# Moving the query scales, merging the copies of key scales, and writing out the order in which an attention opens

## The chip, the cores and the metric

The kernel runs on one core of a Trainium2 chip. The core has five engines that run side by side and wait for each other by semaphores: TensorE (PE; PEld is its weight load), VectorE (DVE), ScalarE (ACT), GpSimd (POOL) and SyncE (SP). DMA transfers are issued from queues on SP, POOL and ACT. The metric is the device time of one execution in microseconds (us). For the kernel before, three runs gave 2776.56, 2783.22 and 2783.88; the median is 2783.22. One more execution was recorded by the profiler.

## The reference, cut to what matters

The model is one block of a perceiver: cross attention to a long context, causal self attention, and a gated feed-forward layer with 4-bit weights. The change touches the cross attention. There, 512 rows of queries (4 x 128 tokens) meet 8192 keys (4 x 2048), in 16 heads of 64 columns, with queries, keys, values and attention weights rounded to integers:

```python
q = (x @ Wq + bq).reshape(1, B * N, H, hd)
kv = (cond @ Wkv + bkv).reshape(1, -1, 2, H, hd)
k, v = (kv[:, :, 0], kv[:, :, 1])
scale = 1.0 / np.sqrt(hd).astype(np.float32)
...
q = _fq_sym(q, axis=-1)          # one scale for each query and head
k = _fq_sym(k, axis=-1)          # one scale for each key and head
v = _fq_sym(v, axis=2)           # one scale for each column
attn = jnp.einsum('bhqd,bhkd->bhqk', q, k)
attn = jax.nn.softmax(attn.astype(jnp.float32), axis=-1)
attn = _fq_unsigned(attn, axis=-1)
out = jnp.einsum('bhqk,bhkd->bhqd', attn, v)
...
return out @ Wp + bp
```

`_fq_sym` divides by a scale (the largest magnitude over 127), rounds, and multiplies back. The kernel keeps the rounded integers and the scales apart.

## The kernel before, in words

The context's 8192 tokens are cut into 64 tiles of 128 tokens (`KT`). A first pass projects them to values (steps 0 to 63), a second pass to keys (steps 64 to 127). One step is one tile: its two halves of 512 columns each take 24 matmuls (`project`, line 364), since every fp32 product is made from three products of split operands. VectorE joins the two accumulators of a half (`join`, lines 378 and 379). In the second pass it then quantises the half (`quantise_k`, by `quantise`: lines 197 to 205): maximum magnitude, scale `sk`, its reciprocal `rs`, and the integers `ki`. SP transposes `ki` by DMA into `kT` (line 630), ScalarE casts that into `kst` (line 644), and POOL stores it to the DRAM buffer `k_d` (line 651).

After every 16 tiles (a key chunk of 2048 keys, four in all) `key_scales` (line 658) turns that chunk's scales into rows: two TensorE transposes (line 663), one for even and one for odd tiles, each into a PSUM tile of its own, a copy from each to `sk_row` (line 665; by ScalarE, for the last chunk by VectorE), and a store to `sk_d` by POOL (line 666). These PSUM tiles come from the same ring of eight as the accumulators.

The order of both passes is written out: `do(step, fn)` puts a piece of work at a step, and `perform()` issues all of it sorted by step, inside `tc.manual_schedule()`, which keeps each engine's instructions in the order of issue. Outside such a block a scheduler places them.

While the last tile of keys is worked on, `open_keys` opens the pool `keys` in the memory of a closed pool, on the right side of the on-chip memory. It holds the keys of a head (`kt`, line 677), the key scales as one row (`sk_half`, line 691) and the same scales spread over all partitions (`sk`, line 696, by POOL). Chunks 0 to 2 are loaded and spread in the written order; the last chunk follows at the opening of the attention (lines 991 to 995), outside the manual block, along with the first load of scale rows for head 1 (`load_rows`, line 833) and the value scales `sv` (line 995). Before these lines, also under the scheduler, the kernel makes `sqs` in the pool `small` from the query scales `sq`: a reciprocal (line 817) and three multiples (line 819). `sqs` gives the exponential its scale and the maximum its operands. An identity matrix is cast to fp16 (line 821).

The attention itself is a written order again: 64 units (16 heads by 4 query tiles), 8 steps of 1024 keys each. In a step TensorE makes scores (line 857), VectorE multiplies them by the spread key scales into `e` and keeps the maximum (line 864). After 8 steps VectorE forms the row's maximum `m` (line 880), ScalarE takes the exponential of `e` in two halves of 4096 (line 898, three buffers of `e`), and later TensorE (line 913) or DMA (line 929) transposes the result, which meets the values (line 962; loaded by POOL, line 827). POOL adds the two sums of the exponentials at the end of a head (line 971).

When the last scores have been issued, `open_projection` (line 1007) closes the pools on the right side, `keys` among them, opens new ones in their place, and has POOL load the first output weights `wp` in two halves (line 1026) and rows of `x` (line 1031). `first_step` (line 1046) begins the output projection with them, between the last transposes and values of the attention:

Of the kernel before, what the change touches and what calls it, by code (L numbers as in the profile page):

```python
# [34 lines left out]
F32 = mybir.dt.float32  # L35
# [5 lines left out]
AF = mybir.ActivationFunctionType  # L41
# [5 lines left out]
P = 128  # L47
B, S, C = 4, 128, 1024
NT = B * S // P
NC = C // P  # L50
H, D = 16, 64
# [3 lines left out]
KT = NK // P  # L55
# [33 lines left out]
def tile_perceiver(  # L89
# [146 lines left out]
    def do(step, fn, *args):  # L236
        agenda.append((step, len(agenda), fn, args))
# [339 lines left out]
    kv = {}  # L577
# [54 lines left out]
    def in_order(t, c):  # L632

        dims = "p h" if len(t.shape) == 3 else "p"
        if c in DMA_KC:
            return t.rearrange(f"{dims} (e n) -> {dims} n e", e=2)
        return t.rearrange(f"{dims} (n e) -> {dims} n e", e=2)
# [20 lines left out]
    def key_scales(c):  # L658

        row = pools["k"].tile([P, 2 * P], F32, name="sk_row", tag="sk_row", bufs=1)  # L660
        for e in range(2):
            pt = kv_ps.tile([P, P], F32, name="sk_pt", tag="ps")
            nc.tensor.transpose(pt, sks[c].rearrange("p h (i e) -> p e h i", e=2)[:, e], ident)
            copy = nc.scalar.copy if c < NKC - 1 else nc.vector.tensor_copy
            copy(in_order(row, c)[:, :, e], pt)
        nc.gpsimd.dma_start(out=sk_d[c].rearrange("h (i n) -> (h i) n", n=2 * P), in_=row)

    kts, sks_at = {}, {}

    def open_keys():  # L670

        early_s.close()
        pools["keys"] = xq.enter_context(tc.tile_pool(name="at_k", bufs=1, side="right"))

    def load_keys(h, c):
        kt = pools["keys"].tile([P, KC // 2], BF16, name=f"kt{h}_{c}", tag="kt", bufs=6)
        nc.sync.dma_start(out=kt, in_=k_d[c][h].rearrange("f d n -> (f d) n"))
        kts[h, c] = kt
# [5 lines left out]
    def load_scales(c):  # L684

        if c == 0:
            sks_at["rows"] = pools["keys"].tile([P, SC], F32, name="sk_half")
        row = sks_at["rows"]
        for half in range(2):
            p = 32 * (2 * (c % 2) + half)  # L690
            nc.sync.dma_start(out=row[p : p + 1, :], in_=sk_d[c][0:1, ts(half, SC)])

    def spread_first(c):
        for half in range(2):
            p = 32 * (2 * (c % 2) + half)
            nc.gpsimd.partition_broadcast(
                tile_of_scales(0, 2 * c + half), sks_at["rows"][p : p + 1, :], channels=P
            )
# [80 lines left out]
    for u in range(first, last):  # L779
        at = TILE * (KT + u)  # L780
        upto = -(-KT * (u + 1 - first) // (last - first))
        for i, v in enumerate(range(done, upto)):
            do(at + 8 + 6 * i, quantise_v, v)
            do(at + 10 + 6.2 * i, store_v, v)
        done = upto
    at = TILE * (2 * KT - 1)
    do(at + 0.2, open_keys)
    for c in range(NKC - 1):
# [19 lines left out]
    with tc.tile_pool(name="at_e", bufs=1) as at_e, tc.tile_pool(  # L808
# [4 lines left out]
        sc_ps = sc_s.enter_context(tc.tile_pool(name="sc_ps", bufs=2, space=PSUM, side="right"))  # L813
        sv = small.tile([P, C], F32, name="sv", tag="sv", bufs=1)

        sqs = small.tile([P, 3, NT, H], F32, name="sqs", tag="sqs", bufs=1)
        nc.vector.reciprocal(sqs[:, 2], sq)
        for i, by in enumerate((1.0, -1.0, -math.log(255.0))):
            nc.vector.tensor_scalar_mul(sqs[:, i], sqs[:, 2] if i == 2 else sq, by)
        ident16 = small.tile([P, P], F16, name="ident16", tag="ident16", bufs=1)  # L820
        nc.scalar.copy(ident16, ident)
        vqs = {}

        def load_values(p, c):
# [163 lines left out]
                scale.tensor_tensor(o, o, r.unsqueeze(2).to_broadcast([P, NT, D]), ALU.mult)  # L988


        load_scales(NKC - 1)
        load_keys(0, NKC - 1)
        spread_first(NKC - 1)
        load_rows(1)
        nc.sync.dma_start(out=sv, in_=sv_d[0].partition_broadcast(P))

        n_steps = len(units) * NSC

# [706 lines left out]
```

## Time and profile before

| what | us |
|---|---|
| median of three runs | 2783.22 |
| the profiled execution | 2784.63 |
| its span | 2782.9 |
| PE busy | 2599.6 (93%) |
| DVE busy | 2402.1 (86%) |
| ACT busy | 1259.2 (45%) |
| POOL busy | 513.5 (18%) |

The span runs from the first to the last recorded instruction of the profiled execution; the rest of its time lies around it. In the profile, "out<-in" names what an instruction writes and reads, L with a number is a line of the kernel before, and brackets after an instruction tell how long its engine stood idle ahead of it and what ended that. Roughly, the queries and values are projected until 750 us, the keys until 1478 us, the cross attention runs until 2100 us, and the rest follows until the end. The mean granted TensorE clock was 0.989 of full speed.

### The profile page before, as it was taken

The page shows a single profiled execution, that of the slowest core. Times are in us where ns is not written, and L with a number is a line of the kernel's source. Part 1 is how long each engine was busy: PE and PEld are TensorE (multiplying, and loading weights), DVE is VectorE, ACT ScalarE, POOL GpSimd, SP SyncE. Part 2 cuts the span into 40 slices and gives each one's busy share as a digit, 9 for nine tenths or more (in the row PEclk, how much of TensorE's full clock was granted, in tenths as well). Part 3 has the DMA queues.
Part 4 walks back from the last instruction along what each step waited for, and adds up shares of the span by engine and source line. Part 5 has one row for each costly group of instructions (what it writes and reads, how often), then busy time and mean ns, then how long its engine had stood idle before and what let it go on. Part 6 is the DMA issues. An engine that isn't in the chain of part 4 may idle for free.

```text
span 2782.9 us, 41479 instructions
## 1 busy us (share of the span) xinstructions
PE 2599.6 (93%) x15496; PEld 2054.8 (74%) x15496; DVE 2402.1 (86%) x3932; ACT 1259.2 (45%) x1404; POOL 513.5 (18%) x715
## 2 busy tenths in 40 slices
PE   8999999999999999999997777777779999899998
PEld 4888888888878788888884555555556777788887
DVE  7999999777899899999878999999995568886685
ACT  4211112222323333333216999999994134333332
POOL 0111111111112222222114333333322000000000
PEclk9999999999999999999998999999999999999999
DMA  6655566788747777777636888888887741133222
GB/s 200 193 201 195 195 232 227 262 296 283 266 109 196 184 190 199 193 192 192 143 84 150 169 171 158 164 158 171 166 156 236 287 156 61 53 99 99 99 93 97
DMA packets 470203, 485.05 MB, mean 174 GB/s; under 512 B 357096, under 2 KB 361768, under 8 KB 470000
## 3 DMA queue, kind: packets, MB, share of 16 engines
q1 hardware_dynamic: 411920, 286.04, 41.2%
q0 software_dynamic: 57024, 195.30, 21.3%
q8 instruction: 122, 2.00, 0.3%
q10 hardware_dynamic: 1056, 1.05, 0.2%
q14 instruction: 81, 0.66, 0.1%
HBM read 256.31 MB, written 140.51 MB: 143 GB/s over the span
## 4 chain that ended last, share of the span: by engine, by line
PE 68%; DVE 24%; issue 4%; DMA 3%; ACT 1%; DVEq 0%; POOL 0%; SPq 0%; ACTq 0%; POOLq 0%
PE kv_a L364 29%; DVE e L864 16%; PE kv_b L364 14%; PE acc_a L1215 4%; PE y_a L1592 3%; PE up_a L180 3%; PE gate_a L180 3%; PE q_ps L314 2%; PE acc_b L1215 2%; PE up_b L180 1%; PE gate_b L180 1%; PE y_b L1592 1%; PE a_pt L913 1%; PE acc_a L1046 1%; DMA sw_d<-ws_d 1%
## 5 line engine op out<-in xcount | busy, mean ns | idle before, releaser
L364 PE MATMUL kv_a<-w_h,c_h 128*128 128x512 f32 x2048 | 798.6, 390 | 0.0
L364 PE MATMUL kv_a<-w_l,c_l 128*128 128x512 f32 x2048 | 797.9, 390 | 0.7 <-ACT w_l L263 0.6
L364 PE MATMUL kv_b<-w_d,c_d 128*128 128x512 f32 x2048 | 797.8, 390 | 0.8 <-DVE c_d L174 0.8
L864 DVE CUSTOM_DVE_ANT_0 e<-sc,sk 128x1024 f32<-128x1024 f32 x512 | 592.0, 1218 | 2.0 <-PE sc L857 1.1
L898 ACT ACTIVATE a<-e,m,sqs 128x4096 int16<-128x4096 f32 x128 | 490.2, 3830 | 5.3 <-DVE m L880 4.9
L364 PEld LDWEIGHTS kv_a<-w_l,c_l 128*128 128x128 f32 x2048 | 385.1, 188 | 81.5 <-ACT w_l L263 1.0
L364 PEld LDWEIGHTS kv_b<-w_d,c_d 128*128 128x128 f32 x2048 | 385.0, 188 | 81.2 <-DVE c_d L174 1.1
L364 PEld LDWEIGHTS kv_a<-w_h,c_h 128*128 128x128 f32 x2048 | 385.2, 188 | 80.3 <-issue 0.2
L857 PE MATMUL sc<-kt,qT 64*128 64x512 bf16 x1024 | 204.6, 390 | 132.8 <-DVE mx L864 131.0
L378 DVE SCALAR_TENSOR_TENSOR f<-kv_a,bkv 128x512 f32<-128x512 f32 x256 | 175.3, 685 | 93.3 <-PE kv_a L364 92.7
L170 ACT ACTIVATE c_h<-c_raw 128x1024 fp32r<-128x1024 f32 x128 | 134.9, 1054 | 224.0 <-PE kv_a L364 199.9
L644 ACT CAST kst<-kT 128x512 bf16<-128x512 int16 x128 | 89.1, 697 | 304.7 <-DMA kT<-ki 304.7
L386 ACT ACTIVATE va<-f 128x1024 f32<-128x1024 f32 x64 | 68.0, 1062 | 302.4 <-DVE f L379 296.7
L857 PEld LDWEIGHTS <-qT 64*128 64x128 bf16 x1024 | 76.9, 93 | 160.6 <-issue 132.9
L379 DVE SCALAR_TENSOR_TENSOR f<-kv_b,f 128x512 f32<-128x512 f32 x256 | 176.5, 689 | 19.2 <-DVE f L378 0.5
L913 PE MATMUL a_pt<-ident,a 128*128 128x128 f32 x1024 | 170.2, 289 | 2.1 <-ACT aT L920 1.3
L837 POOL PARTITION_BROADCAST sk<-sk_row x120 | 142.5, 1299 | 129.7 <-DVE mx L864 129.4
L173 DVE TENSOR_TENSOR c_l<-c_raw,c_h 128x1024 fp32r<-128x1024 f32 x128 | 155.6, 1216 | 9.1 <-ACT c_h L170 9.1
L174 DVE SCALAR_TENSOR_TENSOR c_d<-c_l,c_raw 128x1024 fp32r<-128x1024 f32 x128 | 156.4, 1222 | 3.1
L173 DVE TENSOR_TENSOR fw_l<-fw_raw,fw_h 128x1024 fp32r<-128x1024 f32 x64 | 78.2, 1222 | 91.3 <-ACT fw_h L170 91.3
L913 PEld LDWEIGHTS a_pt<-ident,a 128*128 128x128 f32 x1024 | 109.0, 142 | 61.2 <-issue 42.7
L170 ACT ACTIVATE fw_h<-fw_raw 128x1024 fp32r<-128x1024 f32 x64 | 67.9, 1061 | 165.8 <-PE y_a L1592 69.5
(221 smaller groups left out, 4133.5 us busy)
## 6 DMA issues: line engine op xcount, KB each, us to landing
c_raw<-in_ctxT SPq DMA_DIRECT2D x128, 512.0 KB, 3.8
v_d<-f POOLq DMA_DIRECT2D x64, 512.0 KB, 3.4
vl<-v_d POOLq DMA_DIRECT2D x64, 512.0 KB, 4.5
gu_d<-w_ffn POOLq DMA_DIRECT2D x44, 512.0 KB, 3.2
fw_raw<-gu_d SPq DMA_DIRECT2D x42, 512.0 KB, 3.2
k_d<-kst POOLq DMA_DIRECT2D x128, 128.0 KB, 3.5
vq_d<-vq POOLq DMA_DIRECT2D x32, 512.0 KB, 5.2
kt<-k_d SPq DMA_DIRECT2D x64, 256.0 KB, 6.8
```

What stands on the lines that cost most here:

```text
L170: nc.scalar.mul(hi, src, 1.0 - 0.5 / UP)
L173: nc.vector.tensor_tensor(lo, src, hi, ALU.subtract)
L174: nc.vector.scalar_tensor_tensor(df, lo, -1.0 - UP, src, ALU.mult, ALU.add)
L180: nc.tensor.matmul(ps, lhsT=lhs(i, k), rhs=rhs(i, k), start=(k == 0 and i != 1), stop=(k == NC - 1 and i != 0),)
L364: nc.tensor.matmul(ps, lhsT=tokens[s][i][:, k, :], rhs=w3[s < KT][k][i][:, ts(n, 512)], start=(k == 0 and i != 1), stop=(k == NC - 1 and i ...
L378: nc.vector.scalar_tensor_tensor(f, a, 1.0 + 1.0 / UP, bias[s < KT][n], ALU.mult, ALU.add)
L379: nc.vector.scalar_tensor_tensor(f, b, -1.0 / UP, f, ALU.mult, ALU.add)
L857: nc.tensor.matmul(ps[:, ts(i, 512)], lhsT=qT[rows, h, ts(t, P)], rhs=kts[h, g // 2][rows, ts(g % 2, 512)], start=True, stop=True,)
L864: nc.vector.tensor_tensor_reduce(out=state[n]["e"][-1][:, ts(g % (NSC // NEC), SC)], in0=ps, in1=sks_at[h, g], scale=1.0, scalar=LOWEST, o ...
L898: nc.scalar.activation(a, st["e"][c], AF.Exp, bias=st["m"], scale=sqs[:, 0, t, h : h + 1], accum_out=sums[h][:, t, c : c + 1],)
L913: nc.tensor.transpose(pt[:, i, :], a[:, at_word + P * i : at_word + P * i + P], ident)
L1215: nc.tensor.matmul(ps, lhsT=x3[i][:, t, k, :], rhs=w3s[h, k // 2][i][:, k % 2, :], start=(k == 0 and i != 1), stop=(k == NC - 1 and i != 0),)
```

## The change

There are three edits.

1. `sqs` is made by a new function `scales_of_q`, put into the written order at the step at which the last tile of keys begins. It no longer lies in the pool `small` but in the pool `keys`.
2. `key_scales` makes both transposes into one PSUM tile and copies it to `sk_row` in one instruction.
3. The opening of the attention stands in a `tc.manual_schedule()` block, and after its loads come the cast of the identity and a new exponential of one column into a tile `table`, which makes ScalarE load its table of exponentials there.

```diff
     def key_scales(c):
 
         row = pools["k"].tile([P, 2 * P], F32, name="sk_row", tag="sk_row", bufs=1)
+        pt = kv_ps.tile([P, 2, P], F32, name="sk_pt", tag="ps")
         for e in range(2):
-            pt = kv_ps.tile([P, P], F32, name="sk_pt", tag="ps")
-            nc.tensor.transpose(pt, sks[c].rearrange("p h (i e) -> p e h i", e=2)[:, e], ident)
-            copy = nc.scalar.copy if c < NKC - 1 else nc.vector.tensor_copy
-            copy(in_order(row, c)[:, :, e], pt)
+            nc.tensor.transpose(
+                pt[:, e], sks[c].rearrange("p h (i e) -> p e h i", e=2)[:, e], ident
+            )
+        copy = nc.scalar.copy if c < NKC - 1 else nc.vector.tensor_copy
+        copy(in_order(row, c), pt.rearrange("p e n -> p n e"))
         nc.gpsimd.dma_start(out=sk_d[c].rearrange("h (i n) -> (h i) n", n=2 * P), in_=row)
+
+    def scales_of_q():
+        sqs = kv["sqs"]
+        nc.vector.reciprocal(sqs[:, 2], sq)
+        for i, by in enumerate((1.0, -1.0, -math.log(255.0))):
+            nc.vector.tensor_scalar_mul(sqs[:, i], sqs[:, 2] if i == 2 else sq, by)
 
...
         early_s.close()
         pools["keys"] = xq.enter_context(tc.tile_pool(name="at_k", bufs=1, side="right"))
+        kv["sqs"] = pools["keys"].tile([P, 3, NT, H], F32, name="sqs")
...
         done = upto
+    do(TILE * (2 * KT - 1) + 1, scales_of_q)
     at = TILE * (2 * KT - 1)
     do(at + 0.2, open_keys)
...
-        sqs = small.tile([P, 3, NT, H], F32, name="sqs", tag="sqs", bufs=1)
-        nc.vector.reciprocal(sqs[:, 2], sq)
-        for i, by in enumerate((1.0, -1.0, -math.log(255.0))):
-            nc.vector.tensor_scalar_mul(sqs[:, i], sqs[:, 2] if i == 2 else sq, by)
         ident16 = small.tile([P, P], F16, name="ident16", tag="ident16", bufs=1)
-        nc.scalar.copy(ident16, ident)
+        sqs = kv["sqs"]
+        table = small.tile([P, 1], F32, name="table", tag="table", bufs=1)
...
-        load_scales(NKC - 1)
-        load_keys(0, NKC - 1)
-        spread_first(NKC - 1)
-        load_rows(1)
-        nc.sync.dma_start(out=sv, in_=sv_d[0].partition_broadcast(P))
+        with tc.manual_schedule():
+            load_scales(NKC - 1)
+            load_keys(0, NKC - 1)
+            spread_first(NKC - 1)
+            load_rows(1)
+            nc.sync.dma_start(out=sv, in_=sv_d[0].partition_broadcast(P))
+            nc.scalar.copy(ident16, ident)
+            nc.scalar.activation(table, ident[:, 0:1], AF.Exp)
```

## The prediction

> **What bounds the kernel now.** I read the chain of work that ended last first, then the same chain in order of time around the two places that the change reaches (the start of the attention near 1475 us, its end near 2100 us), then the timeline of each engine there. The first answer says who carries the time as a whole:
>
> ```profile
> PE 68%; DVE 24%; issue 4%; DMA 3%; ACT 1%; DVEq 0%; POOL 0%; SPq 0%; ACTq 0%; POOLq 0%
> ```
>
> Before 1472 us and after 2100 us the chain is almost all TensorE; in the attention it is VectorE (line 864). So microseconds won or lost at a hand-over between stages pass to the end unless a later wait absorbs them. This is VectorE's timeline at the first hand-over (start, duration, then in brackets what it waited for):
>
> ```profile
> 1462.07 0.69 DVE L379 SCALAR_TENSOR_TENSOR f<-kv_b,f 128x512 f32<-128x512 f32 x1
> ...
> 1463.96 0.69 DVE L205 TENSOR_TENSOR ki<-f,rs 128x512 int16<-128x512 f32 x1
> ...
> 1466.71 0.69 DVE L378 SCALAR_TENSOR_TENSOR f<-kv_a,bkv 128x512 f32<-128x512 f32 x1 [2.06 <-PE kv_a L364]
> ...
> 1472.95 0.69 DVE L379 SCALAR_TENSOR_TENSOR f<-kv_b,f 128x512 f32<-128x512 f32 x1
> 1473.56 0.54 DVE L817 RECIPROCAL sqs<-sq 128x64 f32<-128x64 f32 x1
> ...
> 1474.57 0.78 DVE L819 TENSOR_SCALAR sqs<-sq 128x64 f32<-128x64 f32 x2
> 1475.19 1.32 DVE L200 TENSOR_SCALAR sk<-am 128x8 f32<-128x8 f32 x1
> 1476.29 0.26 DVE L819 TENSOR_SCALAR sqs<-sqs 128x64 f32<-128x64 f32 x1
> ...
> 1476.79 0.69 DVE L205 TENSOR_TENSOR ki<-f,rs 128x512 int16<-128x512 f32 x1
> 1477.40 0.48 DVE L665 COPY sk_row<-sk_pt 128x128 f32<-128x128 f32 x2
> 1478.69 1.23 DVE L864 CUSTOM_DVE_ANT_0 e<-sc,sk 128x1024 f32<-128x1024 f32 x1 [0.81 <-PE sc L857]
> ...
> 1493.65 1.23 DVE L864 CUSTOM_DVE_ANT_0 e<-sc,sk 128x1024 f32<-128x1024 f32 x1 [0.86 <-ACT a L898]
> ```
>
> The four scale instructions were drawn between the last half tile's quantisation steps: line 379 to line 205 takes 3.84 us there (1472.95 to 1476.79) and 1.89 us two half tiles earlier (1462.07 to 1463.96). The last line is a stall that starts with ScalarE: its timeline has a 1.28 us load of the exponential's table at 1488.43, after the first maximum. The second hand-over, POOL, ScalarE and TensorE:
>
> ```profile
> 2095.32 1.72 POOL L1026 DMA_DIRECT2D wp<-in_xWp  x2 [15.89 <-DVE m L880]
> 2099.18 3.80 ACT L898 ACTIVATE a<-e,m,sqs 128x4096 int16<-128x4096 f32 x1
> 2102.87 0.20 ACT L898 ACTIVATION_READ_ACCUMULATOR a<-e,m,sqs 128x1 f32 x1
> 2102.92 2.05 PE L1046 MATMUL acc_a<-wp,x 128*128 128x512 f32 x2 [2.69 <-DMA wp<-in_xWp]
> ```
>
> The weights wp are requested as the last maximum ends, fly 7.5 us, and TensorE stands 2.69 us for them. This load is on the chain already, and it starts before the last exponential has run.
>
> **The change, part by part.**
>
> *Scales of queries.* Four instructions leave the last half tile and go after the join before, where VectorE waits 2.06 us for TensorE. They take 0.54 + 0.78 + 0.26 = 1.6 us, less as they overlap, so the gap holds them. The quantisation there ends near 1466.1 instead of 1464.65; its transpose leaves SP at 1467.35, behind two scale loads that wait for POOL, so nothing is late. If the gap were gone the cost would be those 1.6 us at most. In the last half tile line 205 starts 1.95 us earlier, at 1474.84.
>
> *One tile and one copy for key scales.* Two copies of 128 columns took 0.48 us; one took 0.28, a 512-column VectorE pass 0.69, so one of 256 lies between 0.28 and 0.69, by thirds 0.42. Gain 0.06. It starts 0.61 us after line 205, as before: 1475.45 to 1475.87. The second transpose needs sk, ready 1.62 us after line 379 (1474.57), and its 0.49 us end at 1475.1, in time. TensorE's first scores follow 0.06 us after the copy, VectorE's first line 864 0.75 us later: 1476.68 against 1478.69. **-2.0 us.** For the other three key chunks ScalarE makes one copy for two (0.44 us for two); it is off the chain, so I take 0, bounds ±0.4. The ring of eight PSUM tiles then moves by one instead of two; a tile's last user joined some three half tiles (16 us) earlier, so no new wait.
>
> *Table load.* It moves behind the identity copy near 1473.0. Load 1.28 and a one-column activation 0.2 push the two casts of line 644 from 1474.29 to 1475.9. POOL can store those keys only behind the store of the scales, which follows the copy by 0.30 and takes 0.58, so at 1476.75: hidden with 0.9 us to spare. At the first exponential the load is gone, so the 0.86 us stall at 1493.65 goes. **-0.9 us**, bounds 0 and -1.3. In this trace the exponential starts 0.01 us after its load ends (1488.43 + 1.28 to 1489.72), so the load is priced at 1.28. The Trainium skill's page "ScalarE: Activation LUTs", section "What ACT_TABLE_LOAD costs", adds a drain of about 1.38 us to every switch of table. By the page the casts would end near 1477.3, half a microsecond too late, and the sum would be about 0.3 us higher.
>
> *The written opening.* POOL: the first row load for the next head no longer stands before the spread of chunk 2, so these two spreads run about 4 us earlier, hidden. After the last key stores, POOL's order in the built program is: spread 6, the first load of values, spread 7, four row loads, three more loads of values. In the kernel before, both spreads came ahead of that load, which waits until every key store has landed. The last store: quantised half ends 1475.53, cast 3.01 us later as before, ends 1479.16, second store issued 1480.07, lands 3.4 us on (the row's mean there) at 1483.5. Load issue 0.54 and spread 1.25 give 1485.3. VectorE wants spread 7 at 1476.68 + 8.02 = 1484.70: **+0.6 us**. Bounds: over the run key stores land in 2.4 to 7.6 us; 2.4 costs 0, 7.6 costs 4.8. I take the window's own 3.4. The other loads have until 1501 (values) and 1509 (rows). On SP the 512 KB load of sv moves from ahead of the last key transpose (0.35 us of issue, hidden since that transpose waits for VectorE) to behind the last key load; it is first read at 1539.
>
> *What the new place of sqs does at the other end.* sqs now lies in the pool of the keys, which `open_projection` closes before it loads wp into the freed space. So wp must wait for every reader of that pool, and ScalarE's exponentials read sqs. The built program says so: line 1026's load had waits on DMA queues and VectorE; now it also waits for TensorE and ScalarE, up to the second exponential of the last unit, and the POOL sum after it (line 971) has lost its own wait for that exponential. wp is thus issued after 2103.07, at about 2103.1 instead of 2095.32: 7.8 us later. Behind it on POOL are the second half, x and the last sum; on TensorE, in order, the last transposes and values. The flight: 7.47 us in the row. Packets began about 3.2 us after issue; 1 MB at the 385 GB/s seen next would take 2.7, so 5.9 is the low end; the second half took 9.3, the high end. I take 7.47, the same transfer. TensorE then resumes 7.8 us late, having little idle time up to 2140 to give back, and later weight loads are released by TensorE's own progress. **+7.8 us**, bounds 6.2 and 9.6. The granted clock is 0.50 from 2103 to 2106 after the short wait already, so a longer one adds no slow start that was not there.
>
> Sum: -2.0 - 0.9 + 0.6 + 7.8 = +5.5 us. The profiled execution took 2784.63 (span 2782.9), 1.4 above the median of 2783.22; it would take 2790.1, and the median **2788.7**, 0.2% slower.
>
> **The rivals.** 0.3% (8.3 us) is about what a measurement of this kernel can tell from no change.
>
> *Slow side: spread 7 waits long for the key stores.* Against it: the window's 3.4 us. For it: stores up to 7.6 us, and now sv flies with them. At 7.6 us the front gives +4.8 for +0.6, a total of +9.7, 2792.9. It decides past 0.3% from a landing of about 6.3 us.
>
> *The front gains nothing*, because the scales collide in their new gap or the casts come late: +7.8, 2791.0. Against: the gap of 2.06.
>
> *The wait for wp costs nothing*, because TensorE would have been held by the last exponential anyway: -2.3, 2780.9. For: much of the remaining work needs that exponential. Against: TensorE had transposes of the unit's first half ready, and its order puts the wp product ahead of them.
>
> *The opening is not what it says*: a table load reappears before line 898. The built order has none.
>
> **How the numbers follow.** Forecast 0.57; slow stores 0.15; no gain at the front 0.12; wp free 0.12; something else 0.04. Slower by over 0.3% (above 2791.6): the stores' 0.15, half of the no-gain case (it sits at the bound), and 0.05 of the forecast with a 9 us flight: 0.26. Faster by over 0.3% needs 8 us that no row offers: 0.04, since one run of before read 2776.56. Same: 0.70. Range: its low end, 2780.5, takes in the wp-free case, its high end, 2792.9, the slow stores; likeliest case alone (flight 5.9 to 9.3) 2787.1 to 2790.5.
>
> **What would show it.** Right: no sqs line after 1472 us, line 205 about 1.9 us after the last 379, the first line 864 some 2 us earlier, no load at the first exponential; wp issued right behind the last exponential and TensorE idle about 10 us ahead of line 1046. Wrong: wp still issued behind the last maximum, or a stall of several microseconds before the eighth line 864.

## The result, and the profile after

The changed kernel takes 2794.58 us (median of 16 runs, 2790.64 to 2804.5), the kernel before 2785.84 in the same sample (16 runs, 2776.56 to 2793.34): 1.0038 times the time before, 95% interval 1.0026 to 1.005. Of 2785.84 that is 10.6 us slower (7 to 14), where 5.5 were forecast. The forecast of 2788.7 (at most 2792.9) stood on a kernel before of 2783.22; it is 2.6 us above that here. The forecast's range ended at 9.7 us slower. The direction and the place came out as forecast, the size did not. The profiled execution took 2791.5 us, its span is 2789.7 (2784.63 and 2782.9 before). In the changed kernel the lines have moved: 864 is now 871, 880 is 887, 898 is 905, 1026 is 1036, 1046 is 1056, 696 is 705, 827 is 834. The kernels of the experiments each have their own line numbers; the names of the tiles stay.

The chain that ended last, by engine, gives one more percent to DMA and one less to VectorE than before:

```profile
PE 68%; DVE 23%; issue 4%; DMA 4%; ACT 1%; POOL 0%; DVEq 0%; SPq 0%; ACTq 0%; POOLq 0%
```

VectorE's timeline at the first hand-over of the changed kernel (start, duration, in brackets the idle time and what ended it):

```profile
1465.13 0.69 DVE L379 SCALAR_TENSOR_TENSOR f<-kv_b,f 128x512 f32<-128x512 f32 x1
...
1466.57 0.17 DVE L200 TENSOR_SCALAR sk<-am 128x8 f32<-128x8 f32 x1
...
1467.02 0.69 DVE L205 TENSOR_TENSOR ki<-f,rs 128x512 int16<-128x512 f32 x1
1467.63 0.59 DVE L667 COPY sk_row<-sk_pt 128x256 f32<-128x256 f32 x1
1469.03 1.23 DVE L871 CUSTOM_DVE_ANT_0 e<-sc,sk 128x1024 f32<-128x1024 f32 x1 [0.81 <-PE sc L864]
...
1479.41 1.22 DVE L871 CUSTOM_DVE_ANT_0 e<-sc,sk 128x1024 f32<-128x1024 f32 x1 [2.16 <-POOL sk L705]
```

Line 205 follows the last join by 1.89 us, as forecast (3.84 before), and the first line of the attention comes 3.90 us after it (5.74 before). But at the eighth such line VectorE stands 2.16 us for spread 7. POOL and ScalarE there:

```profile
1471.64 1.24 POOL L651 DMA_DIRECT2D k_d<-kst  x2 [1.32 <-ACT kst L644]
1472.91 1.29 POOL L705 PARTITION_BROADCAST sk<-sk_half  x1
1477.49 0.57 POOL L834 DMA_DIRECT2D vq<-vq_d  x1 [3.29 <-PE sc L864]
1478.08 1.30 POOL L705 PARTITION_BROADCAST sk<-sk_half  x1
```

```profile
1465.43 1.28 ACT L1005 ACT_TABLE_LOAD   x1
1466.73 0.20 ACT L1005 ACTIVATE table<-ident 128x1 f32<-128x1 f32 x1
1466.84 1.12 ACT L644 CAST kst<-kT 128x512 bf16<-128x512 int16 x2
...
1481.15 3.80 ACT L905 ACTIVATE a<-e,m,sqs 128x4096 int16<-128x4096 f32 x1 [9.80 <-DVE m L887]
```

Spread 7 stands behind the first load of values, which is issued 5.85 us after the last pair of key stores. The table is loaded early, and the first exponential follows the first maximum directly. The second hand-over, on ScalarE, POOL and TensorE:

```profile
2092.27 3.80 ACT L905 ACTIVATE a<-e,m,sqs 128x4096 int16<-128x4096 f32 x1
```

```profile
2096.46 1.72 POOL L1036 DMA_DIRECT2D wp<-in_xWp  x2 [23.95 <-ACT a L905]
```

```profile
2105.01 2.04 PE L1056 MATMUL acc_a<-wp,x 128*128 128x512 f32 x2 [11.68 <-DMA wp<-in_xWp]
```

The load of wp is released by ScalarE's last exponential, and TensorE stands 11.68 us for it where it stood 2.69.

**One table for all runs.** From the timelines I cut every profiled execution at the same marks: the end of the keys (start of the last join, line 379 of before); A, from there to the second unit's maximum, with which the third unit begins (some expectations below call this the third unit's first maximum); B, to the last maximum; C, from the last maximum to the request of wp; D, from the last maximum to TensorE's first product with it; E, from the last maximum to the first product with the weights `sw` of the next stage; F, from that product to the end of the span.

| kernel | keys end | A | B | C | D | E | F |
|---|---|---|---|---|---|---|---|
| before | 1472.95 | 25.65 | 596.60 | 0.12 | 7.72 | 44.56 | 643.14 |
| before, again | 1466.58 | 25.77 | 596.25 | 0.11 | 7.80 | 43.12 | 647.78 |
| after | 1465.13 | 25.83 | 597.34 | 8.16 | 16.71 | 54.26 | 647.14 |
| after, again | 1465.44 | 25.67 | 597.40 | 8.16 | 16.50 | 54.22 | 644.77 |
| part_scales | 1469.12 | 25.01 | 596.78 | 8.16 | 16.84 | 54.49 | 643.90 |
| part_opening | 1468.75 | 26.32 | 597.05 | 0.12 | 7.90 | 43.26 | 647.72 |
| opening_no_table | 1466.27 | 26.76 | 598.44 | 0.11 | 8.12 | 43.47 | 647.56 |
| opening_sv_first | 1473.18 | 25.01 | 596.88 | 0.11 | 7.66 | 45.88 | 648.85 |
| opening_values_later | 1470.62 | 23.37 | 600.43 | 0.12 | 7.77 | 44.78 | 648.30 |
| part_table | 1468.23 | 25.31 | 596.83 | 0.11 | 8.04 | 44.89 | 643.04 |
| part_table_again | 1472.13 | 25.34 | 596.69 | 0.12 | 7.76 | 44.67 | 643.17 |
| part_copy | 1468.60 | 25.86 | 596.87 | 0.12 | 7.56 | 44.31 | 647.26 |
| part_copy_again | 1470.98 | 25.87 | 597.26 | 0.11 | 7.82 | 43.16 | 644.53 |
| tile_two_copies | 1464.10 | 25.70 | 596.18 | 0.12 | 7.95 | 43.27 | 647.05 |
| copy_last | 1466.22 | 25.87 | 597.11 | 0.11 | 7.81 | 45.01 | 644.49 |
| copy_first_three | 1464.39 | 25.64 | 596.56 | 0.11 | 7.61 | 44.46 | 646.65 |
| exp_scale_apart | 1471.69 | 26.02 | 596.65 | 0.66 | 7.72 | 45.91 | 648.83 |
| apart_values_later | 1466.22 | 23.59 | 596.92 | 0.66 | 7.84 | 44.83 | 648.74 |
| apart_sv_first | 1470.42 | 23.40 | 597.40 | 0.66 | 7.94 | 46.28 | 645.70 |
| apart_old_opening | 1465.31 | 24.80 | 597.86 | 0.65 | 8.27 | 45.18 | 647.65 |

Two columns must be read with care: the end of the keys (1464 to 1473) and F (643 to 649) differ by 6.4 and 4.6 us between the two executions of the kernel before. A, C and D repeat within 0.3 us in the kernels that were traced twice; E lies between 43.1 and 46.3 where the request is early, for a reason given further below. Between the means of two traces each of after and before, A moved by 0.0 us, B by +0.9 and E by +10.4: +11.4 together, against the measured 10.6. The loss is at the second hand-over, and the front, where 2.3 were to be gained, gave nothing.

### The profile page after: what moved, and what is told of

Its sections match the earlier page's. It is cut to its first block, busy times and chain, and to the rows that moved or that the text cites. A ratio compares the mean times of both kernels' runs of the same rounds, so it can differ in the third digit from the quotient of the medians.

```text
span 2789.7 us, 41478 instructions
## 1 busy us (share of the span) xinstructions
PE 2599.5 (93%) x15496; PEld 2054.9 (74%) x15496; DVE 2404.1 (86%) x3931; ACT 1259.7 (45%) x1402; POOL 513.0 (18%) x715
## 3 DMA queue, kind: packets, MB, share of 16 engines
q10 hardware_dynamic: 1056, 1.05, 0.2%
## 4 chain that ended last, share of the span: by engine, by line
PE 68%; DVE 23%; issue 4%; DMA 4%; ACT 1%; POOL 0%; DVEq 0%; SPq 0%; ACTq 0%; POOLq 0%
PE kv_a L364 29%; DVE e L871 15%; PE kv_b L364 14%; PE acc_a L1225 3%; PE y_a L1602 3%; PE up_a L180 3%; PE gate_a L180 3%; PE q_ps L314 2%; PE acc_b L1225 2%; PE gate_b L180 1%; PE up_b L180 1%; PE y_b L1602 1%; PE a_pt L920 1%; PE acc_a L1056 1%; DMA kT<-ki 1%
## 5 line engine op out<-in xcount | busy, mean ns | idle before, releaser
L920 PEld LDWEIGHTS a_pt<-ident,a 128*128 128x128 f32 x1024 | 109.1, 142 | 61.1 <-issue 44.5
L927 ACT COPY aT<-a_pt 128x512 int32<-128x512 int32 x251 | 135.9, 606 | 17.1 <-PE a_pt L920 17.1
```

What stands on the lines that cost most here:

```text
L920: nc.tensor.transpose(pt[:, i, :], a[:, at_word + P * i : at_word + P * i + P], ident)
```

## The experiments

### Is it the wait for wp? The scale of the exponential apart, and the move of the scales alone

The theory: sqs in the pool of the keys makes wp wait for the last exponential, and that is the loss. The rival: the loss lies in F (4 us in the first pair of traces) and in the stall for spread 7. In the first run ScalarE's exponentials read a copy of `sq` in the attention's own pool, so the pool of the keys has no reader on ScalarE at its end:

```diff
+        sq0 = small.tile([P, NT, H], F32, name="sq0", tag="sq0", bufs=1)
...
+            nc.scalar.copy(sq0, sq)
             nc.scalar.activation(table, ident[:, 0:1], AF.Exp)
...
-                scale=sqs[:, 0, t, h : h + 1],
+                scale=sq0[:, t, h : h + 1],
```

> The changed kernel, with one thing more: ScalarE copies the query scales (128x64) into a tile of the attention's own pool as the attention opens, and the exponentials read that copy, so the pool of the keys has no reader on ScalarE left at its end. My theory: nearly all of the loss is the weights wp that wait for the last exponential. Then wp is requested within 0.5 us of the end of the last maximum again (8.3 us in the changed kernel, 0.27 before), TensorE stands about 2.7 us for it instead of 11.7, the stretch from the last maximum to the first product of the next stage falls from 54.4 to about 44.7 us, and the time falls by 9 to 14 us, to the kernel before within 3 us (ratio 0.999 to 1.001). Rival: the loss sits in what follows (647.1 against 643.1 us from that product to the end) and at the opening (spread 7 late by 2.2 us); then the request is early again but the time stays 5 us or more above the kernel before.

Measured: 2787.51 us, 1.0016 of before (1.0004 to 1.0029). The request and TensorE's wait in this kernel (POOL's and TensorE's timelines):

```profile
2095.02 1.72 POOL L1038 DMA_DIRECT2D wp<-in_xWp  x2 [16.44 <-PE a_pt L921]
```

```profile
2102.08 2.04 PE L1058 MATMUL acc_a<-wp,x 128*128 128x512 f32 x2 [2.69 <-DMA wp<-in_xWp]
```

ScalarE is gone as the releaser, the wait is 2.69 us again, and E falls from 54.2 to 45.9. Its ratio lies 0.0022 below that of the changed kernel, some 6 us (from two samples). That settles the mechanism, but the time does not return to within 3 us of before, as was expected: 4.5 us stay.

The second run adds only edit 1 to the kernel before:

```diff
+        kv["sqs"] = pools["keys"].tile([P, 3, NT, H], F32, name="sqs")
...
+    do(TILE * (2 * KT - 1) + 1, scales_of_q)
...
-        sqs = small.tile([P, 3, NT, H], F32, name="sqs", tag="sqs", bufs=1)
-        nc.vector.reciprocal(sqs[:, 2], sq)
...
+        sqs = kv["sqs"]
```

> The kernel before, with the query scales alone moved: made as the last tile of k begins, in a tile of the pool of the keys. Every other instruction stands where it stood. My theory: the request of wp moves behind the last exponential (about 8 us after the last maximum), the stretch from the last maximum to the first product of the next stage grows by 9 to 10 us, and the first line of VectorE in the attention comes about 1.9 us earlier after the last join: 7 to 8 us slower than before in all (ratio 1.0025 to 1.003). If the stage that follows is 647 us instead of 643 here too, the late wp costs those 4 us as well, and the ratio is about 1.004. Rival: wp is not what costs the time; then 2 us faster than before (ratio 0.999).

Measured: 2791.17 us (five runs), 1.0031 (1.0019 to 1.0043), that is +8.6 us, and every mark is that of the changed kernel from C to E. POOL's request of wp again comes behind ScalarE's last exponential. F is 643.90, so the late wp need not lengthen F. So one edit, the place of 768 bytes per partition, carries the loss.

At the front this run contradicts the prediction. A is only 0.7 us shorter, not 2. VectorE's and POOL's timelines of this kernel:

```profile
1470.57 0.89 DVE L200 TENSOR_SCALAR sk<-am 128x8 f32<-128x8 f32 x1
...
1471.73 1.28 DVE L205 TENSOR_TENSOR ki<-f,rs 128x512 int16<-128x512 f32 x1
```

```profile
1469.58 0.54 POOL L838 DMA_DIRECT2D sk_row<-sk_d  x1 [4.41 <-PE sk_pt L663]
1470.14 2.47 POOL L703 PARTITION_BROADCAST sk<-sk_half  x2
```

The four scale instructions are gone from the last half tile, yet line 200 takes 0.89 us instead of 0.17 and line 205 takes 1.28 instead of 0.69, because two of POOL's spreads run at the same time, held back by a row load that waits ahead of them.

### The opening, with and without its parts

The written opening and the table load, added to the kernel before (first diff); then the opening without the table (its last line left out); then the first again with the load of `sv` written ahead of the block, which puts it ahead of the last transpose of keys on SP, where it was (second diff):

```diff
-        nc.scalar.copy(ident16, ident)
...
+        with tc.manual_schedule():
+            load_scales(NKC - 1)
...
+            nc.sync.dma_start(out=sv, in_=sv_d[0].partition_broadcast(P))
+            nc.scalar.copy(ident16, ident)
+            nc.scalar.activation(table, ident[:, 0:1], AF.Exp)
```

```diff
+        nc.sync.dma_start(out=sv, in_=sv_d[0].partition_broadcast(P))
         with tc.manual_schedule():
...
-            nc.sync.dma_start(out=sv, in_=sv_d[0].partition_broadcast(P))
```

> The kernel before, with the written opening and the early load of the exponential's table alone. My theory: no table load before the first exponential and no stall of 0.86 us behind it (0.9 us gained), spread 7 behind the first load of values, which costs 0 to 2.2 us there: between 1 us faster and 1.5 us slower, ratio 0.9996 to 1.0006, and nothing else moves: wp requested 0.3 us after the last maximum, some 643 us from the first product of the next stage to the end. Rival: the opening carries part of the loss of the changed kernel; then 3 us or more slower (ratio above 1.001).

> The kernel before with the written opening alone, without the early table load. Step by step: spread 7 stalls VectorE for about 2.2 us as in the run with the table, and the load of the table stays at the first exponential. The two lie behind one another, so part of the later stall (0.86 us) may be swallowed; the third unit's first maximum 26 to 27.5 us after the last join, 0.5 to 2 us slower than before (ratio 1.0000 to 1.0008). Rival: the order of transfers in the opening also costs 2 to 4 us far behind, where the weights of the last stage are loaded; then ratio 1.001 to 1.002.

> The kernel before with the written opening and the early table load, as in the run of the opening alone, but with the load of sv issued ahead of the last transpose of keys again, as in the kernel before: on SP's queue the order is that of the kernel before, one transfer apart from the run of the opening alone. If the place of sv in SP's queue is what makes the last stretch longer: 643 to 644 us there, two waits for the rotated tiles. If the order on POOL or the table does: 647 to 649. If chance: either. The stall for spread 7 (2.4 us) should be shorter if sv's transfer slowed the key stores, and the same if it did not. Time between 2 us faster and 3 us slower than before.

Measured: 1.0008 (0.9997 to 1.002), 1.0012 (1.0 to 1.0024) and 1.0014 (1.0005 to 1.0024), each a little above the range that was expected. F is 647.56 without the table and 648.85 with sv early, so neither of these makes F long. In the first, VectorE's timeline ahead of the attention has the scale instructions still in the last half tile, and yet:

```profile
1470.56 0.17 DVE L200 TENSOR_SCALAR sk<-am 128x8 f32<-128x8 f32 x1
...
1471.00 0.69 DVE L205 TENSOR_TENSOR ki<-f,rs 128x512 int16<-128x512 f32 x1
...
1472.90 1.23 DVE L864 CUSTOM_DVE_ANT_0 e<-sc,sk 128x1024 f32<-128x1024 f32 x1 [0.82 <-PE sc L857]
```

The first line of the attention comes 4.15 us after the last join (5.74 before): most of what the changed kernel gained there comes from the opening, which takes the row load from ahead of two spreads, so that they end before the last half tile. Then the stalls for spread 7: 2.39 us here, 2.67 without the table, 2.16 and 2.00 in the two traces of the changed kernel, and 1.24 with sv issued early. The first value load follows the last key stores by 5.7 to 6.1 us where sv's transfer flies with them, and by 4.66 where it does not. From its issue, the last key store lands in 4.3 to 4.7 us in the first case and in 3.3 in the second; the load of values is issued some 0.7 us behind that landing.

Without the table, the stall of 0.86 us at the first exponential is there in full behind the other: the two add up.

### Spread 7 set free

The loads of the first values are written behind the spreads and the row loads. First in the changed kernel with the scale apart, then the same with sv issued early (as in the second diff above), then in the kernel before with only the opening and the table:

```diff
             load_rows(1)
+            for c in range(NKC):
+                load_values(0, c)
...
-                if s == 1:
-                    for c in range(NKC):
-                        load_values(0, c)
```

> As the run with the exponential's scale in a tile of its own, and the four loads of the first values written behind the spreads and the row loads of the opening, so that spread 7 no longer stands behind a load that waits for every key store. My theory: spread 7 runs right behind spread 6, VectorE's stall of 2.16 us before its eighth line of the first unit is gone, and the first line of the third unit comes 23.5 to 24 us after the last join of the keys (25.83 in the changed kernel, 25.65 before). The time is some 2 us under the run it is built on, which the trace can show and the times hardly; 2 to 3 us under the kernel before (ratio 0.999). Rival: the row loads, now ahead, wait for the same key stores, and the values come late instead: a wait of the first products of values for their load, and nothing gained.

> The changed kernel with the exponential's scale in a tile of its own, the spreads ahead of the first values, and the load of sv ahead of the last transpose of keys. By theory the front then has all its gain (third unit's first maximum some 23.5 us after the last join, 25.65 before) and wp is requested early. If the place of sv makes the last stretch longer, that is 643 to 644 us here, and the time is 2 to 3 us under the kernel before (ratio 0.999). If the rest of the opening or chance does, it may be 647 to 649 and the time 1 to 3 us above (ratio 1.0005 to 1.001).

> The kernel before with the written opening and the early table load, the four loads of the first values written behind the spreads and row loads; scales of queries and key-scale copies as before. By the steps: both spreads of chunk 2 run ahead of VectorE's last half tile (first line of the attention 4.1 us after the last join, 5.74 before), no stall for spread 7, none for the table: third unit's first maximum 23.4 to 24.0 us after the last join (25.65, 25.77 before): 1.8 to 2.2 us faster, ratio 0.999 to 0.9995, and wp early (0.1 us after the last maximum). Rival: kernels with the written opening lose 2 to 4 us in the stage of the next weights; then 1.000 to 1.001 here too.

POOL's timeline of the first:

```profile
1474.01 2.46 POOL L705 PARTITION_BROADCAST sk<-sk_half  x2
1476.30 2.00 POOL L841 DMA_DIRECT2D sk_row<-sk_d  x4
1478.66 2.11 POOL L835 DMA_DIRECT2D vq<-vq_d  x4 [0.35 <-issue]
```

Both spreads run in one go, there is no stall for them, and A is 23.59, 23.40 and 23.37 us: 2.1 to 2.3 below before, which is the size that the prediction expected of the front. The times: 1.0006 (0.9996 to 1.0016), 1.0015 (1.0004 to 1.0026) and 0.9992 (0.9981 to 1.0002). Only the last, which has neither the moved scales nor the merged copy, comes out where its front says (2.3 of 2780.6 us would be 0.9992), though its one trace has long stretches elsewhere: B holds 3.6 us of waits for scores, and F is 648.30.

### The table load alone

```diff
         nc.scalar.copy(ident16, ident)
+        table = small.tile([P, 1], F32, name="table", tag="table", bufs=1)
+        nc.scalar.activation(table, ident[:, 0:1], AF.Exp)
```

> The kernel before with the early load of the exponential's table alone (one activation on a column, behind the copy of the identity); every other instruction stands as before. Step by step: the stall of 0.86 us at the first exponential goes, so the third unit's first maximum comes 24.8 us after the last join (25.65 and 25.77 in the two traces of before). Time: 0.9 us faster, which the times cannot show (ratio 0.9990 to 1.0005). Rival: the early table is what makes the kernels with the written opening some 2 to 4 us slower than their stages at the front say; then ratio 1.0008 to 1.0015.

> The kernel with the early table load alone, once more. If its 0.9992 and its last stretch of 643 us belong together and to the kernel: again 0.999 to 0.9995 with 643 to 644 us. If the stretch is chance: 643 to 649 us here, and a ratio between 0.999 and 1.0005.

Measured: 0.9992 (0.9982 to 1.0001) and 1.0008 (0.9998 to 1.0018), together no change that the times can show. In the traces the stall of 0.86 us is gone, but A falls by 0.4, not 0.9, for VectorE now waits for scores (its timeline):

```profile
1490.53 1.23 DVE L866 CUSTOM_DVE_ANT_0 e<-sc,sk 128x1024 f32<-128x1024 f32 x1 [0.18 <-PE sc L859]
1492.12 1.23 DVE L866 CUSTOM_DVE_ANT_0 e<-sc,sk 128x1024 f32<-128x1024 f32 x1 [0.35 <-PE sc L859]
```

### What varies by itself

Both kernels once more, unaltered:

> The kernel before, unaltered, for a second trace of it. Question: which stretches vary from run to run by themselves. In the six traces so far the last join of the keys ends anywhere from 1465 to 1473 us, and the stage from its first product to the end takes 643 to 644 us in the two kernels with the old opening and 647 to 649 us in the four with the written one. If the opening sets the second stretch: 643 to 644 us here again, with two waits for the rotated tiles (6.5 us). If chance sets it: it may be 647 to 649 here, with a third such wait. The end of the keys may fall anywhere in 1465 to 1473 by either.

> The changed kernel, unaltered, for a second trace of it. If the opening sets the last stretch: 647 to 649 us from the first product of the next stage, three waits for the rotated tiles. If chance: 643 to 644 is possible. In both, wp requested about 8.2 us after the last maximum, TensorE's first product with it 16.7 us after it, the next stage's first product 54 to 55 us after it, and VectorE's stall for spread 7 about 2.2 us.

Measured: 2781.31 and 2789.23 us (one run each). F is 647.78 in the kernel before and 644.77 in the changed one, the reverse of the first pair, and the keys of before end at 1466.58 instead of 1472.95. So neither the 7.8 us that the keys seemed to gain in the first pair, nor the 4 us that F seemed to lose, can be put down to the change from that pair. What lies behind the two sizes of F can in part be read in the second trace of before, on VectorE and POOL:

```profile
2189.48 0.76 DVE L1277 TENSOR_TENSOR rot<-f,cs 128x256 f32<-128x256 f32 x2
...
2196.72 2.89 DVE L1277 TENSOR_TENSOR rot<-f,cs 128x256 f32<-128x256 f32 x2
2199.65 1.65 DVE L1283 TENSOR_TENSOR f<-f,cs 128x512 f32<-128x512 f32 x1
2201.33 1.63 DVE L1286 TENSOR_TENSOR f<-f,rot 128x512 f32<-128x512 f32 x1
```

```profile
2196.61 5.81 POOL L1157 TENSOR_TENSOR x<-x,row 128x512 f32<-128x512 f32 x4 [62.20 <-DMA row<-in_abo]
```

POOL's four additions meet VectorE's rotation, which takes 6.2 us instead of 2.1, and TensorE waits a third time for the rotated tile (2.92 us). In the first trace they start later against VectorE and slow only the last of the three lines and the next first one. In the second trace the weights `sw_l` and `sw_d` of that product landed late (waits of 0.79 and 0.78 us ahead of it), in the first only `sw_d` did (0.78); that such a microsecond decides which of the two happens is a guess.

This third wait of TensorE, near 2205 us, stands in all sixteen traces with an F of 644.49 or more (0.9 to 3.0 us) and in none of the four with less. Those four (the first of before, part_scales, both of part_table) have the old opening and separate tiles for the key scales of the first three chunks. Of the six traces of such kernels four lie below 644 (mean 644.3 over all six), of the other fourteen none (mean 647.2). So F can be long in the kernel before too, but an edit may well change how often it is. This grouping was made after the runs, and no run tests it.

### The merged copy, and its parts

Edit 2 alone, added to the kernel before:

```diff
-            copy(in_order(row, c)[:, :, e], pt)
...
+        copy(in_order(row, c), pt.rearrange("p e n -> p n e"))
```

> The kernel before with both transposes of key scales in one tile and one copy, alone. Step by step: at the front 0.06 us gained (third unit's first maximum 25.6 us after the last join); ScalarE's three other copies of 256 columns take 0.37 us each for two of 0.26 to 0.28, which lies beside other work: ratio 0.9995 to 1.0005. Rival: it changes when the keys end, through ScalarE's casts or the ring of eight PSUM tiles: then the keys end outside the 1465 to 1473 us of the other traces, and the time goes with it.

> The kernel with the merged copy alone, once more. If its 1.0016 is a property of the kernel: again 1.0008 or more, with the last stretch at 647 us or above as in its first trace. If it was chance of the sample (executions of one kernel spread over some 15 us): nearer 1.000, the last stretch anywhere between 643 and 649 us.

Measured: 1.0016 (1.0006 to 1.0026) and 1.0015 (1.0006 to 1.0023), some 4 us slower, from an edit priced at nothing. Three runs take it apart: the shared tile with two copies, the edit in the last chunk alone, the edit in the other three alone.

```diff
+        pt = kv_ps.tile([P, 2, P], F32, name="sk_pt", tag="ps")
         for e in range(2):
-            pt = kv_ps.tile([P, P], F32, name="sk_pt", tag="ps")
...
+        for e in range(2):
+            copy(in_order(row, c)[:, :, e], pt[:, e])
```

```diff
+        if c == NKC - 1:
...
+        else:
+            for e in range(2):
+                pt = kv_ps.tile([P, P], F32, name="sk_pt", tag="ps")
```

(the second with `c == NKC - 1`, the third with `c < NKC - 1`; inside the condition stands edit 2, behind it the old code).

> The kernel before with both transposes of key scales in one PSUM tile, but still copied in two halves. The merged copy alone was measured 4 us above before twice (1.0016, 1.0015), though its stages at the two hand-overs are those of before. If the ring of eight PSUM tiles, which moves by one per chunk instead of two, is what costs: ratio 1.001 to 1.002 here too. If ScalarE's single copy of 256 columns is: 0.9995 to 1.0005.

> The kernel before with the merged tile and copy in the last chunk of keys alone, on VectorE. The stages there changed by 0.1 us (copy 0.59 us for two in 0.48). Ratio 0.9995 to 1.0005 unless the cost of the merged copy sits at the hand-over to the attention, which then shows as 1.001 or more.

> The kernel before with the merged tile and copy in the first three chunks of keys alone, on ScalarE. If the cost sits in the key stage (ring or ScalarE's copies): ratio 1.001 to 1.002, as with all four. If at the last chunk or in chance: 0.9995 to 1.0005.

Measured: 1.0014 (1.0002 to 1.0026), 1.0003 (0.9991 to 1.0014), 1.0019 (1.0008 to 1.003). So the cost goes with the shared tile in the first three chunks, not with the single copy and not with the hand-over.

This is a tendency of samples, not a clean effect. Take from each sample's difference to before the change of its A (for the kernels with an early request of wp): the eight samples with the shared tile in the first three chunks come out 2.9 to 6.5 us slower (mean 4.4), the seven without it between 1.8 us faster and 4.6 us slower (mean 1.4). opening_sv_first has the 4.6 us without any shared tile. So about 3 us go with the tile, and one sample that is 4 us off proves nothing by itself.

Where the cost sits is not found. F is long (646.6 to 647.7) in four of the five traces with that shared tile and the old opening, and 644.5 in the fifth. But the profiled executions of tile_two_copies and copy_first_three (2778.07 and 2779.57 us) are 6.8 and 5.1 us shorter than their medians, so they do not hold what is to be explained. That the ring of accumulator tiles is what carries it is a guess.

### Everything but the opening

The changed kernel with the old opening, the table load, and the scale apart:

```diff
-        with tc.manual_schedule():
-            load_scales(NKC - 1)
...
+        nc.scalar.copy(ident16, ident)
+        nc.scalar.copy(sq0, sq)
+        nc.scalar.activation(table, ident[:, 0:1], AF.Exp)
...
+        load_scales(NKC - 1)
```

> The changed kernel with the opening as it was (not written out: spreads ahead of the first values, sv ahead of the last transpose of keys), the early table load kept, and a copy of the query scales for the exponentials in a tile of the attention's pool. By the steps: VectorE's first line some 2 us earlier after the last join, no stall for spread 7 and none for the table: the third unit's first maximum 23.2 to 23.9 us after the last join (25.65), wp requested early, so 2 to 2.5 us faster than before (ratio 0.9985 to 0.9995). If the kernels built on the changed one lose 2 to 4 us elsewhere whatever the opening, it is 1.0000 to 1.001.

Measured: 1.0007 (0.9996 to 1.0018), A 24.80. The spreads run beside the last half tile again (line 200 takes 0.89 us), so the front gains 0.9 us of the 2 to 2.5 expected: the expectation had not yet taken in what part_scales showed. The time of the merged copy goes the other way. No run beats the kernel before by more than the times can tell; opening_values_later is nearest to it.

## Why the prediction was wrong

*wp waits for the last exponential (+7.8 us).* The mechanism was right, and its size was 2.6 us too small: E grew by 10.4. The request moved by 8.0 us, as forecast. The first flight was 8.4 and 8.2 us in the two traces, instead of 7.5 and 7.6 before, for the same transfer; that makes D +8.8 (mean of two). Why the flight was longer is not shown. The remaining 1.6 us come from the step "a longer one adds no slow start that was not there", and that step failed. The windows behind the wait (window, then busy time and count of PE, PEld, DVE, ACT, POOL, the granted TensorE clock, DMA share, GB/s) show half the clock for some 4.5 us in the changed kernel,

```profile
2105.00:2107.00 2.00, 1.99 (x3) 0.86 (x4) 0.00 (x0) 0.00 (x0) 0.00 (x0) 0.50 1.02 393
2107.00:2109.00 2.00, 2.00 (x14) 1.56 (x13) 0.69 (x1) 0.00 (x0) 0.00 (x0) 0.50 0.72 289
2109.00:2111.00 2.00, 2.00 (x15) 0.84 (x14) 0.00 (x0) 0.00 (x0) 0.82 (x1) 0.88 0.04 14
```

and for some 3 us in the first trace of before:

```profile
2103.00:2105.00 2.00, 2.00 (x4) 0.86 (x5) 0.00 (x0) 0.07 (x1) 0.62 (x3) 0.50 1.07 397
2105.00:2107.00 2.00, 2.00 (x15) 1.37 (x14) 0.69 (x1) 0.00 (x0) 0.00 (x0) 0.74 1.01 392
```

The second trace of before shows what that row could not: behind a wait of 2.77 us its clock stayed at 1.00. The clock accounts for all of E's differences beyond D, half a microsecond for each microsecond at half the clock. Five traces keep the full clock, and there E is D plus 35.3 to 35.4 us. Nine traces, the first of before among them, have some 3 us at half the clock: D plus 36.8 to 37.2. Three have some 6 us: D plus 38.2 to 38.3. The waits of these seventeen are all 2.5 to 3.2 us, so their length does not tell the three apart. Behind the waits of 11.5 to 11.8 us all three traces have 4.5 to 4.8 us at half: D plus 37.6 to 37.7. So the long wait did add a slow start: 0.7 us more than in the trace that the prediction read, 1.6 more than the mean of the two. Against the mean of all seventeen traces with an early request (44.5), E grew by 9.7 us.

*Scales of queries (-2.0 us).* This step failed, though its number nearly came true by luck. The first line of the attention came 1.84 us earlier behind the last join, and line 205 by 1.95, but edit 1 is not what moved them: alone it moves that first line by 0.6 us, and the opening alone, with the scales in place, by 1.6. The price was read from the difference of two half tiles (3.84 against 1.89 us) and all of it put down to the four instructions. The same fence held a sign of the other cause: line 200 with 1.32 us for eight columns (0.17 two half tiles earlier), line 819 with 0.78 for two. POOL's timeline of the kernel before has the cause itself, two spreads from 1473.97 to 1476.49:

```profile
1473.97 2.52 POOL L696 PARTITION_BROADCAST sk<-sk_half  x2
```

The spreads' move was priced as "hidden"; it was the gain. A row that is nearly eight times its usual length is a reason to ask what ran beside it.

Here the Trainium skill would have helped. "SBUF — State Buffer", section "Who interferes with whom", says that VectorE and GpSimd share a pair of ports, that a VectorE `tensor_scalar`, or an instruction with two inputs from that memory, can be held by a GpSimd instruction that reads it, and that a reduction cannot. The rows agree: beside a spread, lines 200 and 205 took 0.89 to 1.33 and 1.28 us, while the maximum of line 197 stayed at 0.69 and the reciprocal of line 202 at 0.20.

*Table load (-0.9 us).* Gone as forecast, worth 0.4: the step did not say what is late next, which is the scores (0.18 and 0.35 us). On the question of the drain behind a load the trace decides: the activation starts 0.02 us after the load's end (1465.43 + 1.28 to 1466.73) and the casts at 1466.84, and the cast ahead of the load ends where the load starts (1465.13 + 0.30), so the 1.38 us of the page "ScalarE: Activation LUTs", section "What ACT_TABLE_LOAD costs", appear on neither side.

*Spread 7 (+0.6 us).* Inside its bounds (0 to 4.8), but 2.0 to 2.2 us. The landing of the last key store was taken as 3.4 us from its issue, and it was 4.5 and 4.3 us: sv flies with it, and with sv early it was 3.3 and the stall 1.2 us shorter. Another 0.7 us lie between that landing and the issue of the load of values, which the sum left out. The bound of 7.6 us for a landing was misread: it is that of the loads of `kt` from `k_d`; the stores themselves landed in 2.4 to 6.3 us over the run of the kernel before, and 6.3 would have cost 3.5, not 4.8. The prediction named sv as a reason for its slow-stores rival and did not price it.

*One tile and one copy (-0.06 at the front, 0 elsewhere).* At the front +0.1: the copy of 256 columns took 0.59 us, not 0.42. Elsewhere "0, bounds ±0.4" and "no new wait" failed by measurement, by some 4 us when alone, for a reason that stays open. These do not simply add: 11.4 from the stages and 4 from here would be 15, and the whole measured 10.6 (7 to 14). The two samples of the table load strayed from before by -0.0008 and +0.0008, so a part of the 4 us may be the scatter between samples.

*Rivals.* "The front gains nothing" came true, but by spread 7, not by scales in their gap. "wp free" is excluded by part_scales. The sum in terms of the forecast: -2.3 at the front became 0.0, for the most part by spread 7 (1.5 us more than priced) and the table (0.5 less gained), and +7.8 became +10.4.

## What to carry to other kernels

A tile's home is part of the schedule: placed in a pool whose memory is reused at the next hand-over, a table of scales makes the next weights wait for its last reader, 8 us here, however early it was written. When a row takes several times its usual length, look first at what the neighbouring engine does at that moment, before the time is put down to the instructions around it. One pair of traces is not enough to say where a few microseconds went: a second trace of each unaltered kernel showed that 7.8 and 4 us of "effects" also occur without any edit.

## What was not expected of the hardware

A POOL spread or addition beside VectorE lengthens some of VectorE's instructions several times over (line 200: 0.17 to 1.33 us; the rotation in the next stage: 2.1 to 6.2 us for its three lines), and whether the two meet depends on when a transfer lands. Behind waits of TensorE of 2.5 to 3.2 us at one and the same place, the granted clock was never at half, for some 3 us, or for some 6 (five, nine and three traces), which moves the end of the stage by up to 3 us; behind waits of 11.5 to 11.8 us it was half for 4.5 to 4.8 us in all three. And a PSUM tile shared by two transposes, in the first three chunks of a stage of 700 us, went with 4 to 5 us more in four samples of kernels that differ from before in nothing else but its copies; no trace shows where, and scatter of that size also occurs without it.
